# Transposing attention probabilities by halves of the queries, in a kernel that runs a Mamba block beside a local transformer

## The chip, the cores and the metric

The kernel runs on one core of a Trainium2 chip. A core has a matrix engine (TensorE, PE in the profile), a vector engine (VectorE, DVE), an activation engine (ScalarE, ACT), a general engine (GpSimd, POOL) and a sync engine (SyncE, SP) that here issues nearly all transfers. Each engine works through its own queue in order and they meet through semaphores. PE writes to PSUM, eight banks of 512 fp32 columns on 128 partitions; DVE and ACT read and write it[...]. The metric is the device time of one execution in microseconds.

## The reference: what is computed

The input is 4096 tokens of width 256, in fp32. After a layer norm, two independent branches read the same tokens, and the output is their sum with the input:

```
xn = layernorm(x)
x  = x + mamba(xn) + transformer(xn)
```

The Mamba branch widens to 512 channels, convolves over four tokens, and computes for each channel and each of 16 states a linear recurrence over all tokens:

```
h[t] = exp(dt[t]*A) * h[t-1] + dt[t]*xc[t]*B[t]
y[t] = sum over the 16 states of C[t] * h[t]
```

and then `(y + xc*D) * silu(z) @ out_proj`.

The transformer branch has two layers with eight heads of 64. Queries and keys are normalized and rotated. Each window of 128 queries sees its own 128 keys and the 128 before them, under a mask, with a softmax over the at most 256 keys. `attn @ v` and an output projection are added to the stream; a gated GELU network of hidden width 682 follows.

## The kernel before, in words

Everything is fp32. The tokens are cut in 16 steps of 256 for the transformer (so 32 steps over both layers, two windows of 128 in each) and in 8 blocks of 512 for Mamba (four channel groups of 128 in each). One transformer step is the unit of time of the schedule, and one channel group of Mamba runs beside each step.

**The order.** The program first only records its pieces of work with `add(engine, us, emit, reads, writes, soon=...)`. A piece has a key: the step in which it is wanted, less its `soon` (its lead, in steps). `Plan.order` (line 183) then plays all five engines through with the written durations and, on each engine that falls free, picks the ready piece with the smallest key, among those whose key is no more than `AHEAD` steps beyond the oldest piece that isn't done. A piece has to find its buffers free. On PE the planner charges `SWITCH` (0.1) for going from one shape of the array to another (`part`: whole array, "rows" or "columns"), and prefers a piece of the present shape if its key is within `NEAR`. What comes out is one fixed program order for each engine, and so for each queue, SP's among them. `late` in a transfer is its size in KB.

**Mamba's recurrence** (`recur`, line 775) is called for each block b, channel group c and group g of two states, g from 0 to 7. It loads B and C of the two states, broadcast to all partitions, into two tiles of the six-tile buffer `bc` (SP, two transfers of 512 KB). POOL multiplies dt*xc into B for both states at once (line 793). For each state ACT forms the decay in a PSUM tile `da` (line 802), DVE scans (line 807), ACT keeps the last column (line 813), DVE multiplies by C (line 817). Then the states are summed over. If g is in `PAIRED`, POOL adds the two states of the group (line 825) and PE transposes one tile of 128x512 into the bank `y`, as four accumulating 128x128 transposes against the identity (line 829, `collect`). Otherwise PE does so for both states, in eight. `close` (line 842) takes `y` back after all eight groups.

**Attention** (`attend`, line 996) is called for each window, and `pair(g)` in it for each four heads, g being 0 or 1. `score` (line 1017) multiplies queries and keys with the contraction over 64, so heads j = 0 and 1 lie in the upper and the lower half of the array's rows and write to two banks. DVE adds the mask and takes the maximum (line 1032), ACT forms the exponentials and their sums (line 1042). That leaves P with queries on the partitions, in tiles `prs[j]` of 128 queries by two heads (i) by 256 keys. To multiply by V it is needed with the keys on the partitions. So for each i PE transposes four 128x128 pieces into one bank (line 1055), ACT copies the bank to a tile `prT` (line 1059), and after both i `mix` (line 1071) multiplies, with the two heads j in halves of the array's columns. An fp32 product is two matmul instructions on PE; a transpose is one.

PSUM's banks are shared: five for all matmul outputs (`banks`, "mm"), two for the decays, one for `y`.

The rest that the text names: projections L918 and L635, their rotation L945 to L985, the network's matmuls L1176, L1239 and L1258, Mamba's step sizes L734 and output projection L879.

Of the kernel before, what the change touches and what calls it, by code (L numbers as in the profile page):

```python
# [22 lines left out]
ALU = mybir.AluOpType  # L23
# [19 lines left out]
AHEAD = 2.190000  # L43
# [5 lines left out]
PAIRED = (1, 3, 5, 7)  # L49
# [269 lines left out]
def mamba_and_local_transformer(  # L319
# [45 lines left out]
    probs_T = buffer("prT", 4, [P, 2, 2, P])  # L365
# [89 lines left out]
    def load_small():  # L455
        dma(96, lambda: xpw.ap, lambda: xp_wT.rearrange("(c p) n -> p c n", p=P), writes=[xpw], soon=-0.27)
        for at_row in (0, DH):
            dma(32, lambda at_row=at_row: dtw.ap[at_row : at_row + DTR], lambda: dt_wT, writes=[(dtw, at_row)], soon=-1.3)
        dma(128, lambda: b2row.ap, lambda: b2_d[DEPTH - 1 : DEPTH, :].partition_broadcast(P), writes=[b2row], soon=-0.91)

    def load_qkv(l):
        for s in range(3):
            cut = slice(s * INNER, (s + 1) * INNER)
            dma(
                512, lambda cut=cut: wqkv.ap[:, :, cut],
                lambda cut=cut: wqkv_d[l][:, cut].rearrange("(k p) n -> p k n", p=P), writes=[(wqkv, s)], soon=-0.18,
            )

    def load_rest(l):
        dma(512, lambda: wo.ap, lambda: wo_d[l].rearrange("(h p) n -> p h n", p=P), writes=[wo], soon=-0.99)  # L470
        for half in range(2):
            for m, n in ((0, WHOLE), (NM - 1, LAST)):
# [4 lines left out]
                    writes=[(w1, (half, m))], soon=0.35,  # L477
# [4 lines left out]
            lambda: w2_d[l][0:whole, :].rearrange("(m p) n -> p m n", p=MC), writes=[(w2, 0)], soon=-0.25,  # L482
        )
        dma(42, lambda: w2.ap[0 : HID - whole, NM - 1, :], lambda: w2_d[l][whole:HID, :], writes=[(w2, 1)], soon=0.66)
# [28 lines left out]
        add("PE", 8.3, shift, [w1], [pb], soon=-0.7)  # L513
        add("DVE", 0.4, bias, [pb], [b1, b1x], soon=0.6)
        add("DVE", 4.6, scale, [], [w1], port=True, soon=0.34)
# [14 lines left out]
    def base_of(s):  # L530

        base = plan.value(rows_b)
        if s in sums:
            dma(256, lambda: base.ap, lambda: sums[s].ap, [sums[s]], [base], soon=-0.57)
            return base
        dma(256, lambda: base.ap, lambda: rows(x, s), writes=[base], soon=-1.31)
# [3 lines left out]
            ), [b2row], [base], soon=-0.48,  # L540
# [3 lines left out]
    def finish(s, po, base):  # L544

        add("DVE", 0.6, lambda: nc.vector.tensor_tensor(base.ap, halves(po), base.ap, ALU.add), [po], [base], soon=-1.48)  # L546
        if s in sums:
            dma(256, lambda: rows(out, s), lambda: base.ap, [base], soon=-0.51)
            return
        sums[s] = plan.fixed(dram.tile([P, NW, D], F32, tag=f"sum{s}", name=f"sum{s}"))  # L550
        dma(256, lambda: sums[s].ap, lambda: base.ap, [base], [sums[s]], soon=0.0)
# [4 lines left out]
    def shift_column(l, s):  # L556
        now = xts[l, s]
        if s == 0:
            add("POOL", 0.14, lambda: nc.gpsimd.memset(now.ap[:, 1, 0:1], 0.0), [], [(now, 0)], soon=0.0)
        else:  # L560
# [3 lines left out]
                [(old, 1)], [(now, 0)], soon=-0.52,  # L564
            )

    def normalize(s):
# [5 lines left out]
        dma(256, lambda: xb.ap, lambda: rows(x, s), writes=[xb], soon=0.37)  # L573
# [27 lines left out]
        add("DVE", 1.1, stats, [xb], [mv], soon=1.29)  # L601
        add("ACT", 0.5, root, [mv], [rstd], soon=0.53)
        add("DVE", 0.6, centre, [mv, rstd], [xb], port=True, soon=-0.03)
        now = xts[0, s] = plan.value(tokens)
        add("PE", 0.44, turn, [xb], [pt], holds=[now], soon=0.01)
        add("ACT", 0.48, lambda: nc.scalar.copy(now.ap[:, :, 1:], halves(pt)), [pt], [(now, 1)], soon=0.16)
        shift_column(0, s)
        dma(256, lambda: xn_d[s].ap, lambda: now.ap[:, :, 1:], [(now, 1)], [xn_d[s]], soon=-0.93)
# [3 lines left out]
    def reload(s):  # L612
        now = xts[1, s] = plan.value(tokens)
        dma(256, lambda: now.ap[:, :, 1:], lambda: x1_d[s].ap, [x1_d[s]], [(now, 1)], soon=-1.46)
        shift_column(1, s)
# [5 lines left out]
    def in_half(i):  # L621
# [3 lines left out]
            lambda: in_wT[:, i * DI : (i + 1) * DI].rearrange("(k p) n -> p k n", p=P), writes=[w], soon=-1.21,  # L625
# [3 lines left out]
    def in_proj(b, w, c, to):  # L629
# [9 lines left out]
        add("PE", 1.72, emit, [w, xms[b]], [pm], holds=[to], soon=-0.6)  # L639
        return pm  # L640

    def front_load(b):
        xm = xms[b] = plan.value(xms_b)
        for i in range(PB):
            s = b * PB + i
            dma(
                256, lambda i=i: xm.ap[:, :, i * TS : (i + 1) * TS], lambda s=s: xn_d[s].ap, [xn_d[s]], [(xm, i)], soon=0.29
# [5 lines left out]
    def front_conv(b, c, w):  # L653
        xin, xc, tail = plan.value(rows_m), xcs[b], tails[b]
        edge = slice(c * (TAPS - 1), (c + 1) * (TAPS - 1))
        if b == 0:
            add("POOL", 0.14, lambda: nc.gpsimd.memset(xin.ap[:, 0 : TAPS - 1], 0.0), [], [(xin, 0)], soon=0.12)
        else:
# [3 lines left out]
                [(old, c)], [(xin, 0)], soon=0.95,  # L662
            )
        pm = in_proj(b, w, c, xin)
        add("ACT", 0.48, lambda: nc.scalar.copy(xin.ap[:, TAPS - 1 :], pm.ap), [pm], [(xin, 1)], soon=0.73)
        if b < NB - 1:
            add(
                "POOL", 0.14, lambda: nc.gpsimd.tensor_copy(tail.ap[:, edge], xin.ap[:, TB:]), [(xin, 1)], [(tail, c)], soon=0.09
# [5 lines left out]
            ), [], [pm], soon=-0.15,  # L674
# [8 lines left out]
        for j in range(TAPS - 1):  # L683
            add("DVE", 0.7, lambda j=j: tap(j), [xin, pm], [(xc, c) if j == TAPS - 2 else pm], soon=0.78)

    def silu(v):
# [4 lines left out]
        add("ACT", 4.52, emit, [], [v], soon=0.43)  # L691

    def front_dbl(b):
# [3 lines left out]
        def emit():  # L697
# [9 lines left out]
        add("PE", 1.75, emit, [xc, xpw], [px], holds=[xd, part], soon=-0.32, part="columns")  # L707
        add("ACT", 0.48, lambda: nc.scalar.copy(part.ap[0:n, 0:TB], px.ap[DH : DH + n]), [px], [part], alone=[px], soon=0.25)
        add(
            "DVE", 0.6, lambda: nc.vector.tensor_tensor(xd.ap[0:n], px.ap[0:n], part.ap[0:n, 0:TB], ALU.add),  # L710
            [px, part], [(xd, 0)], alone=[px], soon=-1.5,
        )

        add("ACT", 0.48, lambda: nc.scalar.copy(xd.ap[DH : DH + DTR], xd.ap[0:DTR]), [(xd, 0)], [(xd, 1)], soon=-0.07)
        xds[b] = xd
        bc = bcs[b] = plan.fixed(dram.tile([2 * NS, TB], F32, tag=f"bc{b}", name=f"bc{b}"))
        dma(64, lambda: bc.ap, lambda: xd.ap[DTR:n, :], [(xd, 0)], [bc], soon=0.15)

    def gate_conv(b, c, w):
# [4 lines left out]
        add("ACT", 0.48, lambda: nc.scalar.copy(sz.ap[:, c, :], pz.ap), [pz], [(sz, c)], soon=-0.62)  # L724

    def times(b, c):
# [12 lines left out]
        add("PE", 1.15, emit, [xd, dtw], banks2, holds=dts2, soon=0.77, part="rows")  # L739
        for i in range(2):  # L740
# [3 lines left out]
                ), [banks2[i]], [dts2[i]], soon=0.17,  # L744
# [3 lines left out]
    def prepare(b, c):  # L748

        if c % 2 == 0:  # L750
# [7 lines left out]
        add("ACT", 0.6, lambda: nc.scalar.activation(e.ap[:, n], dt.ap, AF.Abs), [dt], [e], soon=-0.79)  # L758
        add("ACT", 0.6, lambda: nc.scalar.activation(dt.ap, dt.ap, AF.Relu), [], [dt], soon=-1.5)
        add("ACT", 0.54, lambda: nc.scalar.activation(e.ap[:, n], e.ap[:, n], AF.Exp, scale=-1.0), [], [e], soon=1.42)  # L760
        add(
            "DVE", 0.36, lambda: nc.vector.tensor_scalar(r.ap[:, n], e.ap[:, n], 1.0, -1.0, ALU.add, ALU.add),
            [e], [r], port=True, soon=0.0,
        )
        add("POOL", 1.22, lambda: nc.gpsimd.tensor_tensor(r.ap[:, n], e.ap[:, n], r.ap[:, n], ALU.subtract), [e], [r], soon=0.43)
        add("ACT", 0.6, lambda: nc.scalar.activation(e.ap[:, n], e.ap[:, n], AF.Ln, bias=one_t), [], [e], soon=0.53)
        add("POOL", 1.22, lambda: nc.gpsimd.tensor_tensor(dt.ap, dt.ap, r.ap[:, n], ALU.add), [r], [dt], soon=-1.5)
        add("POOL", 1.22, lambda: nc.gpsimd.tensor_tensor(dt.ap, dt.ap, e.ap[:, n], ALU.add), [e], [dt], soon=-0.88)
        add(
            "DVE", 0.61, lambda: nc.vector.tensor_tensor(dtx.ap, dt.ap, xc.ap[:, c, :], ALU.mult),  # L770
            [dt, (xc, c)], [dtx], port=True, soon=0.42,
# [3 lines left out]
    def recur(b, c, g):  # L775
# [6 lines left out]
        for s in range(2):  # L782
# [4 lines left out]
                .rearrange("n t -> (n t)").partition_broadcast(P), [bc], [w], soon=-0.78,  # L787
# [7 lines left out]
            ), [dtx], [u], soon=0.16,  # L795
# [618 lines left out]
```

## Time and profile before

| what | value |
|---|---|
| runs | 1903.18 us median of 3 (1902.42 to 1904.25) |
| the profiled execution | 1899.32 us |
| its span, first to last instruction | 1897.5 us |
| granted TensorE clock | 0.993 |
| median matmul record, L829, L1055, L1017 | 273, 273, 272 ns |
| median weight-load record, L829 and L1055 / L1017 | 141 / 188 ns |
| POOL's sum, L825: count, mean | 128, 1287 ns |
| transfer of two states' B or C: size, issue to landing | 512 KB, 4.4 us |

Times come from one profiled execution. A group's row gives the line of the kernel, the engine, the operation, its output and inputs by name, the shape, the count, the time in which at least one of them ran, the mean of one, and the idle time ahead of them on their engine with what ended it. A matmul record lasts from its start to its modelled end; the next one starts before that, so what a matmul costs PE is read from start to start.

### The profile page before, as it was taken

Reading aid. Unit: us, or ns where it says so; the run is one execution under the profiler, and the core shown is the slowest. Engines: PE = TensorE matmul, PEld = TensorE weight load, DVE = VectorE, ACT = ScalarE, POOL = GpSimd, SP = SyncE. Lnnn points to the kernel's source line nnn. Section 1 sums busy time; section 2 is a strip of 40 time slices with the busy share of each in tenths; the row PEclk is TensorE's granted clock in tenths of the full one; section 3 lists DMA queues with packets and bytes.
Section 4 is the critical chain, followed back from the end, with each engine's and each line's share of the span. In section 5 each row is a group of like instructions: output and inputs, shape, how many; then the busy total and the mean of one; then the engine's idle time right before and its main releaser. Section 6 shows DMA issues by size and latency. Waiting matters only on the chain. (4 is left out here: it accounts for less than half of the span.)

```text
span 1897.5 us, 35612 instructions
## 1 busy us (share of the span) xinstructions
PE 1855.4 (98%) x12432; PEld 1423.5 (75%) x12432; DVE 1724.6 (91%) x3190; ACT 1539.9 (81%) x3634; POOL 1410.9 (74%) x1178
## 2 busy tenths in 40 slices
PE   7999999999999999999999999999999999999997
PEld 4777777877777778778778787778777787777786
DVE  6799999999998999989998898998999989998996
ACT  5897988888878788788886888888898878888773
POOL 3676888777877778867787676887768877787874
PEclk9999999999999999999999999999999999999998
DMA  5453655554555455555555644556444564544654
GB/s 188 139 194 114 221 166 180 180 173 166 198 167 182 145 170 194 163 187 185 191 184 191 216 152 162 169 189 222 152 160 163 191 214 159 180 160 155 217 173 144
DMA packets 133956, 334.69 MB, mean 176 GB/s; under 512 B 13468, under 2 KB 57200, under 8 KB 133776
## 3 DMA queue, kind: packets, MB, share of 16 engines
q1 hardware_dynamic: 133488, 332.21, 52.5%
q8 instruction: 98, 1.61, 0.3%
q14 instruction: 82, 0.67, 0.1%
q10 hardware_dynamic: 288, 0.20, 0.0%
HBM read 315.06 MB, written 17.30 MB: 175 GB/s over the span
## 5 line engine op out<-in xcount | busy, mean ns | idle before, releaser
L793 POOL TENSOR_TENSOR bc<-dtx,bc 128x1024 f32<-128x1024 f32 x256 | 606.0, 2369 | 144.1 <-DMA bc<-bc 107.1
L807 DVE TENSOR_TENSOR_SCAN da<-da,state,bc 128x512 f32<-128x512 f32 x448 | 563.5, 1278 | 39.7 <-ACT da L802 21.1
L802 ACT ACTIVATE da<-dt,negA 128x512 f32<-128x512 f32 x512 | 348.3, 693 | 78.4 <-DVE bc L817 74.9
L918 PE MATMUL mm<-wqkv,xt 128*128 128x512 f32 x768 | 355.1, 598 | 1.4 <-DVE top L1032 1.2
L817 DVE TENSOR_TENSOR bc<-da,bc 128x512 f32<-128x512 f32 x512 | 339.0, 678 | 5.7 <-ACT state L813 3.4
L1176 PE MATMUL mm<-hn,w 128*128 128x256 f32 (+1 forms) x1408 | 338.2, 383 | 1.3 <-DVE mlp L1226 0.5
L1176 PEld LDWEIGHTS mm<-hn,w 128*128 128x128 f32 (+1 forms) x1408 | 256.8, 189 | 60.2 <-issue 17.0
L1042 ACT ACTIVATE pr<-pr,top 128x256 f32<-128x256 f32 (+1 forms) x512 | 253.2, 500 | 25.9 <-DVE top L1032 25.6
L918 PEld LDWEIGHTS mm<-wqkv,xt 128*128 128x128 f32 x768 | 139.5, 191 | 133.4 <-issue 120.7
L825 POOL TENSOR_TENSOR bc<-bc 128x512 f32<-128x512 f32 x128 | 164.6, 1287 | 88.0 <-DVE bc L817 86.9
L829 PE MATMUL y<-ident,bc 128*128 128x128 f32 x1536 | 214.9, 277 | 8.8 <-POOL bc L825 8.3
L1032 DVE CUSTOM_DVE_ANT_0 pr<-mm,maskf,nrm 128x256 f32<-128x256 f32 (+1 forms) x512 | 213.1, 474 | 9.5 <-PE mm L1017 9.0
L985 POOL TENSOR_TENSOR turn<-turn,trig 128x512 f32<-128x512 f32 x128 | 162.9, 1293 | 65.7 <-DVE turn L978 57.1
L829 PEld LDWEIGHTS y<-ident,bc 128*128 128x128 f32 x1536 | 175.5, 142 | 46.6 <-issue 20.8
L945 POOL TENSOR_TENSOR turn<-turn,turn 128x512 f32<-128x512 f32 x128 | 164.6, 1286 | 51.3 <-DVE turn L963 50.8
L1017 PEld LDWEIGHTS mm<-kT,qT 64*128 64x128 f32 x2016 | 119.9, 187 | 36.1 <-issue 14.4
L1059 ACT COPY prT<-mm 128x512 f32<-128x512 f32 (+1 forms) x256 | 137.0, 591 | 7.0 <-PE mm L1055 6.3
L1055 PE MATMUL mm<-ident,pr 128*128 128x128 f32 x1008 | 135.7, 278 | 3.8 <-ACT qT L956 1.4
L813 ACT COPY state<-da 128x1 f32<-128x1 f32 x448 | 70.1, 165 | 85.1 <-DVE da L807 70.3
L1017 PE MATMUL mm<-kT,qT 64*128 64x128 f32 x2016 | 136.7, 281 | 0.0
L1071 PE MATMUL mm<-prT,v 128*64 128x128 f32 x2016 | 132.2, 278 | 0.7 <-ACT prT L1059 0.2
L1055 PEld LDWEIGHTS mm<-ident,pr 128*128 128x128 f32 x1008 | 117.6, 144 | 18.9 <-issue 4.9
(132 smaller groups left out, 3444.9 us busy)
## 6 DMA issues: line engine op xcount, KB each, us to landing
bc<-bc SPq DMA_DIRECT2D x512, 512.0 KB, 4.4
io<-in_x SPq DMA_DIRECT2D x32, 256.0 KB, 5.0
mw<-in_in_wT SPq DMA_DIRECT2D x16, 512.0 KB, 5.1
rot<-in_rot SPq DMA_DIRECT2D x32, 128.0 KB, 4.2
xn<-xt SPq DMA_DIRECT2D x16, 256.0 KB, 4.0
xm<-xn SPq DMA_DIRECT2D x16, 256.0 KB, 4.2
x<-mid SPq DMA_DIRECT2D x16, 256.0 KB, 3.0
mw<-in_out_wT SPq DMA_DIRECT2D x8, 512.0 KB, 3.7
```

Of the source, the lines that this page charges most:

```text
L793: "POOL", 2.35, lambda: nc.gpsimd.tensor_tensor(u.ap, dtx.ap.unsqueeze(1).to_broadcast([P, NG, TB]), u.ap, ALU.mult), [dtx], [u], soon=0.16,
L802: "ACT", 0.63, lambda h=h, n=n: nc.scalar.activation(h.ap, dt.ap, AF.Exp, scale=negA[:, c * NS + n : c * NS + n + 1]), [dt], [h], soon=0.96,
L807: "DVE", 1.18, lambda h=h, n=n, i=i: nc.vector.tensor_tensor_scan(h.ap, h.ap, u.ap[:, i, :], state.ap[:, c, n : n + 1] if b else 0.0, ALU. ...
L817: "DVE", 0.61, lambda h=h, i=i: nc.vector.tensor_tensor(u.ap[:, i, :], h.ap, spread[1].ap[:, i, :], ALU.mult), [h, spread[1]], [(u, i)], a ...
L825: add("POOL", 1.22, lambda: nc.gpsimd.tensor_tensor(u.ap[:, 0, :], u.ap[:, 0, :], u.ap[:, 1, :], ALU.add), [], [u], soon=-0.37)
L829: nc.tensor.matmul(y.ap[:, t, :], lhsT=u.ap[:, i, t * P : (t + 1) * P], rhs=ident, is_transpose=True, start=g == 0 and i == 0 and t == 0, ...
L918: nc.tensor.matmul(pm.ap, lhsT=hT[k], rhs=wqkv.ap[:, k, q * INNER : (q + 1) * INNER], start=k == 0, stop=k == KC - 1,)
L1017: nc.tensor.matmul(halves(scs[j])[:, i, a * WIN : (a + 1) * WIN], lhsT=qT.ap[half, 2 * g + i, :], rhs=kk.ap[half, 2 * g + i, :], start=n == 0,
L1032: nc.vector.tensor_tensor_reduce(out=prs[j].ap[:, i, keys], in0=halves(scs[j])[:, i, keys], in1=mask[:, keys], scale=nrm.ap[:, h : h + 1], ...
L1042: nc.scalar.activation(prs[j].ap[:, i, keys], prs[j].ap[:, i, keys], AF.Exp, bias=top.ap[:, h : h + 1], scale=-1.0, accum_out=den.ap[:, h ...
L1055: nc.tensor.transpose(ppv()[:, j, a, :], prs[j].ap[:, i, a * WIN : (a + 1) * WIN], ident)
L1176: nc.tensor.matmul(halves(pm)[0:r, i, :], lhsT=w1.ap[:, k, c0 : c0 + r], rhs=hn.ap[:, k, :], start=k == 0, stop=k == KC - 1,)
```

## The change

Three things change together.

1. **P's transposes.** Both i are done in one piece of work. Each 128x128 transpose is split by the queries, which are P's partitions, in two halves r = 0 and 1. A half takes 64 rows of P against a 64x64 part of the identity and gives 128 keys by 64 queries. The halves lie in different row halves of the array and write to two banks, one for each r. So there are sixteen transposes where there were eight, and the piece is of the shape "rows". ACT copies each bank to its half of the queries in one joint tile `prT`, in runs of 64 columns; that buffer is two tiles of twice the size instead of four.
2. **Six groups.** `PAIRED` holds 0, 1, 3, 4, 5 and 7 instead of 1, 3, 5 and 7.
3. **Leads.** `AHEAD` goes from 2.19 to 2.4, and nearly every `soon` has a new value between -1.5 and 1.5. They change no instruction, only the order.

```diff
-AHEAD = 2.190000
+AHEAD = 2.400000
...
-PAIRED = (1, 3, 5, 7)
+PAIRED = (0, 1, 3, 4, 5, 7)
...
-    probs_T = buffer("prT", 4, [P, 2, 2, P])
+    probs_T = buffer("prT", 2, [P, 2, 2, 2, P])
...
-            add("PE", 1.0, score, [qT] + [kk for _, kk, _ in pieces], scs, holds=prs, soon=0.88, part="rows")
+            add("PE", 1.0, score, [qT] + [kk for _, kk, _ in pieces], scs, holds=prs, soon=0.64, part="rows")
...
-            prTs = []
-            for i in range(2):
-                pp, prT = plan.value(banks), plan.value(probs_T)
-                ppv = lambda pp=pp: pp.ap.rearrange("p (j a q) -> p j a q", j=2, a=2)
-
-                def turn(i=i, ppv=ppv):
+
+            pps, prT = [plan.value(banks) for _ in range(2)], plan.value(probs_T)
+            ppv = lambda r: pps[r].ap.rearrange("p (i j a q) -> p i j a q", i=2, j=2, a=2)
+
+            def turn():
+                for i in range(2):
                     for j in range(2):
                         for a, _, _ in pieces:
-                            nc.tensor.transpose(ppv()[:, j, a, :], prs[j].ap[:, i, a * WIN : (a + 1) * WIN], ident)
-
-                add("PE", 0.44, turn, prs, [pp], holds=[prT], soon=0.02)
+                            for r in range(2):
+                                half = slice(r * DH, (r + 1) * DH)
+                                nc.tensor.transpose(
+                                    ppv(r)[:, i, j, a, :], prs[j].ap[half, i, a * WIN : (a + 1) * WIN], ident[half, half]
+                                )
+
+            add("PE", 0.5, turn, prs, pps, holds=[prT], soon=0.81, part="rows")
+            for r in range(2):
                 add(
-                    "ACT", 0.48, lambda ppv=ppv, prT=prT: nc.scalar.copy(prT.ap[:, :, first:], ppv()[:, :, first:]),
-                    [pp], [prT], soon=0.59,
+                    "ACT", 0.48, lambda r=r: nc.scalar.copy(
+                        prT.ap[:, :, :, first:, r * DH : (r + 1) * DH], ppv(r)[:, :, :, first:, :]
+                    ), [pps[r]], [(prT, r)], soon=1.37,
                 )
 
-                prTs.append(prT)
-
             def mix():
-                for i, prT in enumerate(prTs):
+                for i in range(2):
...
-                                rhs=prT.ap[:, j, a, :],
+                                rhs=prT.ap[:, i, j, a, :],
...
-            add("POOL", 1.22, lambda: nc.gpsimd.tensor_tensor(u.ap[:, 0, :], u.ap[:, 0, :], u.ap[:, 1, :], ALU.add), [], [u], soon=-0.37)
+            add("POOL", 1.22, lambda: nc.gpsimd.tensor_tensor(u.ap[:, 0, :], u.ap[:, 0, :], u.ap[:, 1, :], ALU.add), [], [u], soon=-1.5)
```

## The prediction

> **What bounds the kernel now.** I read the busy shares first, then the busy time by stretch, then the costliest groups, then the matrix engine's timeline around one attention pair, then the waits. Busy time and the forty slices:
>
> ```profile
> PE 1855.4 (98%) x12432; PEld 1423.5 (75%) x12432; DVE 1724.6 (91%) x3190; ACT 1539.9 (81%) x3634; POOL 1410.9 (74%) x1178
> ...
> PE   7999999999999999999999999999999999999997
> ...
> DVE  6799999999998999989998898998999989998996
> ```
>
> PE (TensorE) is full from the second slice to the last but one, so there is no stage to single out: PE time saved anywhere in the middle counts. DVE (VectorE) is close behind it. By stretch (columns: length, busy time with instruction count of PE, PEld, DVE, ACT, POOL, then clock, DMA share, GB/s):
>
> ```profile
> 100.00:500.00 400.00, 392.97 (x2698) 300.24 (x2697) 379.25 (x729) 341.13 (x829) 302.78 (x257) 1.00 0.52 172
> ...
> 900.00:1300.00 400.00, 397.28 (x2631) 305.79 (x2630) 361.27 (x662) 330.50 (x788) 304.76 (x247) 0.99 0.55 182
> ```
>
> Of 400 us DVE is busy 379 in the first and 361 in the other: 95% and 90%. That is the ceiling over every PE saving: if DVE could be driven to 98% everywhere, the stretches from 100 to 1700 us (DVE 1489 us in all) would still take 1520 of their 1600, so no more than some 80 us can be had there.
>
> The groups that the change touches (line, engine, operation, count | busy us, mean ns of one | idle before):
>
> ```profile
> L829 PE MATMUL y<-ident,bc 128*128 128x128 f32 x1536 | 214.9, 277 | 8.8 <-POOL bc L825 8.3
> ...
> L1059 ACT COPY prT<-mm 128x512 f32<-128x512 f32 (+1 forms) x256 | 137.0, 591 | 7.0 <-PE mm L1055 6.3
> L1055 PE MATMUL mm<-ident,pr 128*128 128x128 f32 x1008 | 135.7, 278 | 3.8 <-ACT qT L956 1.4
> ```
>
> The 277 ns is latency from issue to end, and successive matmuls overlap. What one costs is the step from its start to the next one's start, which the timeline of PE gives (start us, length us, line):
>
> ```profile
> 952.94 1.04 PE L829 MATMUL y<-ident,bc 128*128 128x128 f32 x8
> 953.91 1.16 PE L1017 MATMUL mm<-kT,qT 64*128 64x128 f32 x16
> 955.00 0.66 PE L1071 MATMUL mm<-prT,v 128*64 128x128 f32 x8
> 955.59 1.53 PE L829 MATMUL y<-ident,bc 128*128 128x128 f32 x12
> 956.95 5.32 PE L918 MATMUL mm<-wqkv,xt 128*128 128x512 f32 x12
> ```
>
> Within a run of records the start-to-start step of a full 128x128 transpose is 109 ns (median over L829, and over L1055). The scores of L1017 use half the array's rows each. They start in twos, 7 ns apart, and the next two start 112 ns after them: 16 in 8 x 0.112 = 0.893 us, where one after another would be 1.8. So two 64-row matmuls do run side by side here, and so do their weight loads.
>
> The timeline shows a second cost. Eight transposes of L829 should take 8 x 0.109 = 0.87 us, but L1017 starts 0.97 later; L1017 then holds PE for 1.09 instead of 0.893, L1071 for 0.59 instead of 4 x 0.109 = 0.436, and the next L829 takes 1.36 instead of 1.31. Going from whole array to half rows to half columns and back thus cost 0.10 + 0.20 + 0.15 + 0.05 = 0.5 us in three **changes of shape**. Over all records in order of start, I count 368 such changes; against nominal steps the median loss is 0.195 us going into rows and 0.230 going back to the whole array. A separate stretch of row-halved work costs about 0.42 us beside its matmuls. The 144 pieces of such work (128 scores, 16 step sizes of L734) now stand in 102 stretches, 1.41 to a stretch.
>
> **The change, part by part.**
>
> *The transposes of P, removed:* 1008 x 0.109 = 109.9 us of PE. *Added:* 2016 transposes of 64 rows by 128 columns, moving 64 identity columns, in 1008 twos. No row shows such a two. Its nearest row is L1017: the same 64x128 weights in twos, with twice the moving columns, 112 ns. If the columns set the step it is half, 56 ns; if the rate of issue or the loads set it (L1017 never issues four instructions, two loads and two matmuls, faster than in 112), it is 112. The transposes' loads are shorter: their load record is 141 ns in L1055 against 188 in L1017[...]. So I take 60 ns, nearer the low end: 1008 x 0.060 = 60.5 us; ends 56.4 and 112.9.
>
> Here the Trainium skill speaks against the change. Its page "TensorE: Matmul & The Clock Gate", section "Back-to-back issue gap", says that a small matmul has a floor: about 25 ns from start to start, but about 62 ns each where the sequencer's hardware decoding is off. By the 62, sixteen transposes would take 0.99 us a pair against eight at 0.109 = 0.87 now, and the part would lose 128 x 0.12 = 15 us instead of saving 49. The trace's row decides: L1017's sixteen average 56 ns, with 7 between the two of a pair, below that floor, so the 62 isn't in force. By the 25, two take 50, just under the 56 of the columns. The same page, section "LDWEIGHTS (loading the stationary operand)", says that a load takes the time of its columns, however few rows it has. The change therefore doubles the load time. One after another, 16 loads at the 0.107 us that its formula gives for 128 columns are 1.7 us a pair, +107 us in all. In L1017 two loads of 128 columns fit into each 112 ns, so I use the row again.
>
> *Changes of shape, added:* a whole-array transpose stood among other whole-array work for nothing; a half-row one needs the array re-shaped unless another row piece stands beside it. Ends: 0 of the 128 pairs (each falls next to a score) and 128 (each alone). At the present 1.41 to a stretch the 128 would make 91. Some will fall beside scores, which they were never free to do. I take 75: 75 x 0.42 = 31.5 us; ends 0 and 53.8.
>
> *The six groups:* groups 0 and 4 join the paired ones, over 8 blocks x 4 channel groups: 64 times one collect of four L829 transposes goes, 64 x 4 x 0.109 = 27.9 us of PE. GpSimd gets 64 more sums. Their row is L825, 1287 ns: 64 x 1.287 = 82.4 us, so POOL goes from 1411 to 1493 us, still below DVE. Who waits for it:
>
> ```profile
> PE y L829 <- POOL bc L825: 8.3, 3, 3.5
> ...
> DVE da L807 <- POOL bc L793: 12.0, 13, 2.6
> ...
> POOL bc L793 <- DMA bc<-bc: 107.1, 74, 4.9
> POOL bc L825 <- DVE bc L817: 86.9, 42, 6.4
> ```
>
> (us in total, times, longest.) The first line, for 128 sums, becomes 192: +4 us. Behind a sum on POOL's queue stands the next group's product (L793), for which the scan (L807) waits; nothing excludes that each sum delays a scan (82 us), and 0 is the other end. Today 128 sums and all else on POOL cost the scan 12 us; half as many sums more: +5. The cover is the stock of three groups' buffers: the chain from a load's issue (4.4 us) over product (2.4), two scans and their products (about 4), sum (1.3) and collect (0.5) is 12.6 us, and a group comes every 1897.5 / 256 = 7.4, so three last 22 us. Without that slack each sum would put its 1.3 us on the scan.
>
> *Eviction:* still two ACT copies of 512 columns a pair, now written in runs of 64: 591 ns each as L1059; on ACT (81%) a tenth more (14 us) would be hidden. Both wait for the one joint transpose of about 0.5 us instead of 0.44 for the first, and it needs two of the five banks at once; behind it on PE's queue everything waits if the order misjudges that. Taken as 0, ends 0 and +10 (128 x 0.08). The four half-size probability buffers become two of twice the size: nothing.
>
> *Leads, and the limit of 2.4 instead of 2.19 steps:* they re-order every queue, SP's loads and POOL's included, and add no instruction. What they could win is PE's idle time, 1897.5 - 1855.4 = 42 us, of which the first 100 us and the last 48 have some 24; what they could lose isn't bounded by any row. Taken as 0, ends -15 and +20.
>
> **Sum:** -109.9 + 60.5 + 31.5 - 27.9 + 4 + 5 = -36.8, so a span of 1860.7. Around the span lie 1.8 us (1899.3 - 1897.5), so 1862.5 for that execution, which was 3.9 us under the median of the runs: **1866 us**. DVE's 1724.6 us are then 93% of the span, and in the stretch from 100 to 500 some 97%, as full as PE is; that is why I credit nothing for leads.
>
> **Rivals.** *The shape changes cluster away.* If the order puts most transposes next to scores (n = 15 stretches) and POOL's delay stays hidden, PE saves 109.9 - 60.5 - 6 + 27.9 = 71 us, and DVE's ceiling of about 80 hardly lets more through: 1832. For it: the stock of row pieces nearly doubles, from 144 to 272, and stretches of two scores exist already (39 of them). Against: a transpose comes due only after its mask and exponentials, when its score is long past.
>
> *DVE takes over.* PE gives up its time, but DVE with waits for ACT, POOL and PE in its queue does not get above 95% in the middle. The 1600 us stretch becomes 1489 / 0.95 = 1568, with the ends as now: -32. If it stays at 94%, -16, or 1887; with every transpose in its own stretch (another 22 us) it is much the same, 1888. For it: DVE's idle time has many small causes (21 us for ACT's decay, 12 for POOL, 12.5 and 11.4 for PE). I put this case at **1888**. Against: a good part of those waits is for PE, and shrinks with it.
>
> *The twos don't run side by side, and it is slower.* If a two costs 109 ns or more, one matmul after another or issue-bound, the transposes save nothing, and their shape changes are a pure loss: +31.5 - 27.9 + 9 = 13 us, **1916**, with every one alone +35. The point from which this decides: the saving is gone when 1008 x (0.109 - step) equals 31.5 + 9 - 27.9 = 12.6, at a step of 97 ns. For it: no record shows four instructions in less than 112 ns, and the skill's floors. Against: the 7 ns between the two of a pair.
>
> **How the numbers follow.** Likeliest case (1866, its own range 1845 to 1882): 0.50. Clustered, 1832: 0.13. DVE or lone stretches, 1888: 0.19. Not side by side, 1916: 0.18. About 0.2% (3.8 us) is what a measurement can tell from no change. The first two lie wholly on the faster side, the third all but 0.02, and of the last 0.05 falls within 0.2%, 0.13 beyond: faster 0.80, same 0.07, slower 0.13. Half of the clustered case lies below 1832 and some 0.12 above 1908, so the range is 1832 to 1908.
>
> **What would show it.** Right: the new transposes' records step by about 60 ns from two to two, with 7 inside; the PE matmul count rises by 1008 - 256 = 752; PE's stretches of row-halved work rise from 102 to about 177; L825's heir has 192 sums of about 1.29 us, and PE waits for it about 12 us; DVE's share reaches 93%. Wrong: a two at 100 ns or more, stretches above 230 or near 110, scan waits on POOL in the tens of us, or PE's busy share falling well below 97% with DVE no fuller, which would say that the order, and not a unit, sets the time.

## The result, and the profile after

The kernel became slower: 1913.95 us (median of 4, 1913.16 to 1916.57) against 1903.51 before, a ratio of 1.0055 with a 95% interval of 1.0043 to 1.0068. The profiled execution's span is 1912.3 us, 14.8 more than before (some 4 us of these are not in the medians: the execution of before that was profiled was one of the faster ones). My 1866 was wrong, and the time lies above the range.

First the busy shares and slices, of the kernel after:

```profile
PE 1830.8 (96%) x13184; PEld 1359.3 (71%) x13184; DVE 1725.4 (90%) x3190; ACT 1543.8 (81%) x3634; POOL 1482.8 (78%) x1242
...
PE   7999999999999999999989999999999999999986
```

The instruction counts are the forecast ones: 752 more matmuls on PE, 64 more sums on POOL. DVE's work is the same, and its share *fell*, from 91 to 90%. PE is less full than before in a longer span. So nothing took over as a full engine. This is one of the signs of being wrong that I had named: PE's share well below 97% with DVE no fuller. By stretch (columns as before):

```profile
100.00:500.00 400.00, 386.62 (x2817) 285.81 (x2816) 371.20 (x695) 330.42 (x792) 311.33 (x263) 0.99 0.51 167
...
900.00:1300.00 400.00, 388.64 (x2792) 289.09 (x2790) 361.80 (x655) 331.63 (x781) 322.91 (x265) 0.99 0.55 185
```

From 100 to 500 us PE lost 6 us of busy time and VectorE 8: VectorE did not move up to the ceiling that I had set for it.

The groups that changed, of the kernel after (line, engine, operation, shapes, count | busy us, mean ns | idle before):

```profile
L829 PE MATMUL y<-ident,bc 128*128 128x128 f32 x1280 | 180.4, 277 | 19.8 <-POOL bc L825 19.6
...
L1057 PE MATMUL mm<-ident,pr 64*128 64x64 f32 x2016 | 90.4, 229 | 3.4 <-DVE turn L978 1.5 <-ACT pr L1042 1.3 <-DVE mlp L1230 0.3
```

and PE's timeline around one joint piece of transposes (start us, length us, line):

```profile
902.36 0.59 PE L1145 MATMUL mm<-sq,mean_w 128*128 128x256 f32 x2
902.89 0.71 PE L1057 MATMUL mm<-ident,pr 64*128 64x64 f32 x16
903.53 1.15 PE L1075 MATMUL mm<-prT,v 128*64 128x128 f32 x16
904.60 1.98 PE L918 MATMUL mm<-wqkv,xt 128*128 128x512 f32 x4
```

Sixteen half-row transposes hold PE for 903.53 - 902.89 = 0.64 us. By their start times, the two of a pair mostly start 3 or 4 ns apart and the next two 63 ns later (112 after the first two of a piece): 8 x 0.063 = 0.504 us, and the rest belongs to a change of shape. They do run side by side, at the step that I took (60).

**A ledger of PE's time.** I gave every matmul record the time up to the next one's start, and set against it the step of its kind in an unbroken run (whole transpose 109 ns, 256 columns 216, 512 columns 429, half-array work half of its like, a half-row transpose 63 / 2). What a step takes beyond that is put down to a change of shape if it is the step over the change or one of the two after it, else to "elsewhere": waits and other gaps. All in us of one profiled execution:

| kernel | streaming | at changes of shape (number) | elsewhere | before the first and from the last matmul on | span |
|---|---|---|---|---|---|
| before | 1756.6 | 84.3 (361) | 44.4 | 12.2 | 1897.5 |
| after | 1682.3 | 142.3 (578) | 76.2 | 11.5 | 1912.3 |
| difference | -74.3 | +58.0 (+217) | +31.8 | -0.7 | +14.8 |

(My count of 368 changes before had seven more, from the 42-column matmuls of L495, which the ledger takes as whole.) Which three steps count as "at" a change is a choice: with the two steps before a change taken in as well, the differences are +65.6 and +24, with one before and one after it +50.5 and +39. The sum stands; its division is good to some 8 us.

The streaming saved is what I forecast: 109.9 - 63.5 + 27.9 = 74.3 (I had 77.3). Two things ate it: 217 more changes of shape, and waits elsewhere. Stretches of row-halved work went from 102 to 208, where I had taken 177, and those of column-halved work from 90 to 116, of which I had not thought.

### The profile page after: what moved, and what is told of

It is laid out like the page before. It is cut to its first block, busy times and chain, and to the rows that moved or that the text cites. A ratio compares the mean times of both kernels' runs of the same rounds, so it can differ in the third digit from the quotient of the medians.

```text
span 1912.3 us, 37355 instructions
## 1 busy us (share of the span) xinstructions
PE 1830.8 (96%) x13184; PEld 1359.3 (71%) x13184; DVE 1725.4 (90%) x3190; ACT 1543.8 (81%) x3634; POOL 1482.8 (78%) x1242
## 5 line engine op out<-in xcount | busy, mean ns | idle before, releaser
L918 PE MATMUL mm<-wqkv,xt 128*128 128x512 f32 x768 | 362.2, 603 | 3.5 <-DVE turn L965 1.4
L1180 PE MATMUL mm<-hn,w 128*128 128x256 f32 (+1 forms) x1408 | 333.9, 384 | 7.7 <-DVE top L1032 4.2
L825 POOL TENSOR_TENSOR bc<-bc 128x512 f32<-128x512 f32 x192 | 244.4, 1277 | 69.9 <-DVE bc L817 65.6
L1042 ACT ACTIVATE pr<-pr,top 128x256 f32<-128x256 f32 (+1 forms) x512 | 253.3, 500 | 18.2 <-DVE top L1032 17.9
L829 PE MATMUL y<-ident,bc 128*128 128x128 f32 x1280 | 180.4, 277 | 19.8 <-POOL bc L825 19.6
L829 PEld LDWEIGHTS y<-ident,bc 128*128 128x128 f32 x1280 | 144.9, 141 | 54.7 <-POOL bc L825 27.6
L1017 PEld LDWEIGHTS mm<-kT,qT 64*128 64x128 f32 x2016 | 125.7, 189 | 36.0 <-issue 12.4
L1017 PE MATMUL mm<-kT,qT 64*128 64x128 f32 x2016 | 145.1, 284 | 5.6 <-ACT kT L956 2.3
L813 ACT COPY state<-da 128x1 f32<-128x1 f32 x448 | 70.9, 165 | 87.4 <-DVE da L807 71.5
L1075 PE MATMUL mm<-prT,v 128*64 128x128 f32 x2016 | 140.2, 281 | 0.5
L1075 PEld LDWEIGHTS mm<-prT,v 128*64 128x64 f32 x2016 | 113.9, 137 | 27.2 <-issue 8.0
L635 PE MATMUL mm<-xm,mw 128*128 128x512 f32 x256 | 123.2, 608 | 2.0 <-DVE xc L678 1.3
## 6 DMA issues: line engine op xcount, KB each, us to landing
rot<-in_rot SPq DMA_DIRECT2D x32, 128.0 KB, 2.2
```

The source lines that it names most:

```text
L825: add("POOL", 1.22, lambda: nc.gpsimd.tensor_tensor(u.ap[:, 0, :], u.ap[:, 0, :], u.ap[:, 1, :], ALU.add), [], [u], soon=-1.5)
L829: nc.tensor.matmul(y.ap[:, t, :], lhsT=u.ap[:, i, t * P : (t + 1) * P], rhs=ident, is_transpose=True, start=g == 0 and i == 0 and t == 0, ...
L918: nc.tensor.matmul(pm.ap, lhsT=hT[k], rhs=wqkv.ap[:, k, q * INNER : (q + 1) * INNER], start=k == 0, stop=k == KC - 1,)
L1017: nc.tensor.matmul(halves(scs[j])[:, i, a * WIN : (a + 1) * WIN], lhsT=qT.ap[half, 2 * g + i, :], rhs=kk.ap[half, 2 * g + i, :], start=n == 0,
L1042: nc.scalar.activation(prs[j].ap[:, i, keys], prs[j].ap[:, i, keys], AF.Exp, bias=top.ap[:, h : h + 1], scale=-1.0, accum_out=den.ap[:, h ...
L1075: nc.tensor.matmul(hpair(po.ap)[j * DH : (j + 1) * DH, hp, :], lhsT=vv.ap[:, h * DH : (h + 1) * DH], rhs=prT.ap[:, i, j, a, :], start=a == ...
```

## The experiments

**Theory A**: each change of shape costs PE about 0.2 us, and the split pays in them for what it streams less. Against it, **B**: changes hide behind waits and the order's waits took the gain; **C**: GpSimd's 64 more sums did, by late products for the scans; **D**: the leads were set badly, the structure itself is a gain. The expectations also speak of **A+**: A, and a set of leads serves one structure only. Later came **E**: VectorE is the real bound; and **F**: PE, VectorE and the dependences hold each other. Times are medians; the kernel before, run beside each set, stood at 1902.2, 1905.8, 1901.7, 1901.5 and 1902.5 us.

### One cost added: extra changes of shape in the order of before

```diff
                 def turn(i=i, ppv=ppv):
+                    if i == 0:
+                        nc.tensor.transpose(ppv()[:, 0, 1, 0:DH], prs[0].ap[0:DH, 0, WIN:], ident[0:DH, 0:DH])
                     for j in range(2):
```

> The kernel before, its order unchanged, with one extra transpose of 64 rows (0.06 us) put ahead of the first four whole-array transposes of P in each of the 128 pairs; what it writes is overwritten. By the order of PE's work, changes of shape rise from 361 to 613. Theory A (each change of shape costs PE some 0.2 us, and that is where the gain went): 252 x 0.2 + 128 x 0.06 = 58 us more, so about 1960; at least 1940 if PE's own slack takes some. Theory B (changes of shape are hidden behind waits, and the order's waits took the gain): 8 us more at most, 1904 to 1912.

1937.6 us, ratio 1.0173 (1.0149 to 1.0196): 28 to 37 us more, for 4 us of streaming. The ledger: streaming 1760.6, at changes 128.0 (613), elsewhere 34.0. So 252 changes took 43.7 us, 0.17 each, and 10 us of it came out of waits. B falls. A's mechanism stands with a smaller price than I gave it: the time stayed below my "at least 1940". The busy row of this run's page:

```profile
PE 1895.4 (98%) x12560; PEld 1436.5 (74%) x12560; DVE 1729.8 (89%) x3190; ACT 1545.4 (80%) x3634; POOL 1410.8 (73%) x1178
```

Note that 98% is the share of before too: a 64-row transpose and its two changes count as "busy" like useful work.

### The split alone undone, in the order of after

```diff
-                            for r in range(2):
-                                half = slice(r * DH, (r + 1) * DH)
-                                nc.tensor.transpose(ppv(r)[:, i, j, a, :], prs[j].ap[half, i, ...], ident[half, half])
+                            nc.tensor.transpose(ppv(i)[:, j, a, :], prs[j].ap[:, i, ...], ident)
```

> The kernel after with its own order, but P is transposed in whole 128x128 pieces, one bank for each i; leads, six groups and the joint piece stay. Changes of shape fall from 578 to 404, the streaming of the transposes grows by 46 us. Theory A: the two nearly cancel, 174 x 0.2 = 35 to 43 us less against 46 more, so 1914 to 1925. Theory B (changes hidden, PE's time counts): 1955 to 1960. If PE is no longer what sets the time, 1914.

1917.9 us (1916.17 to 1919.45), against 1913.95 for the kernel after (up to 1916.57). The ledger: streaming 1728.7 (+46.4 against after), at changes 105.4 (404; -36.9), elsewhere 71.8 (-4.4). B falls again. With everything else held, order included, the split saves 46 us of streaming, pays 37 for 174 changes, and is worth about 4 us, with ranges that just overlap. The time alone, near 1914, would also fit the third case of the expectation, that PE no longer sets the time.

```profile
PE 1845.0 (96%) x12176; PEld 1396.6 (73%) x12176; DVE 1725.8 (90%) x3190; ACT 1544.0 (81%) x3634; POOL 1482.8 (77%) x1242
```

The run also parts the change in two. It has the whole transposes of before, but the six groups, the joint piece and the order of after:

| part | streaming | at changes | elsewhere | span | forecast |
|---|---|---|---|---|---|
| the split: after, less this run | -46.4 | +36.9 | +4.4 | -5.3 | -17.9 |
| six groups, joint piece, leads: this run, less before | -27.9 | +21.1 | +27.4 | +20.1 | -18.9 |

(What is missing to the span lies at its two ends.) So the split itself did not make the kernel slower. The other part did: I had it at -27.9 + 4 + 5 = -18.9, with nothing for the order.

### The six groups: undone, and their sums shortened

In the first, only `PAIRED` goes back to four groups; its order is made anew by that. In the second the order stays:

```diff
+            many = slice(0, 8 if g in (0, 4) else TB)
-            add("POOL", 1.22, lambda: nc.gpsimd.tensor_tensor(u.ap[:, 0, :], u.ap[:, 0, :], u.ap[:, 1, :], ALU.add), ...)
+            add("POOL", 1.22, lambda: nc.gpsimd.tensor_tensor(u.ap[:, 0, many], u.ap[:, 0, many], u.ap[:, 1, many], ALU.add), ...)
```

> The kernel after with PAIRED 1, 3, 5, 7 again; its leads were set with six groups, so the order changes too. If the six groups' saving on PE of 28 us is real: about 1940. If GpSimd's sums cause the waits: 1900 or less. If the leads fit one structure only, the order gets worse on top: 1940 to 1960.

> The kernel after with its own order; GpSimd's sums of the two added groups (0 and 4) take 8 of the 512 columns, so that part of the states' sum is left out, and POOL has 64 x 1.2 = 77 us less to do. Theory A and a fault of the order alike: the wait of PE for the sums (19.6 us) shrinks to some 10, the time falls by 5 to 12 us, to 1902 to 1909. Theory C (GpSimd's queue took the gain, by late products for the scans): 25 us less or more, below 1890.

Four groups: 1946.8 us, 33 more than after; the ledger has streaming +27.9, changes +2.5, elsewhere -1.8. Here the streaming put back came through whole, in an order made anew. Short sums: 1909.8 us, 4 less, with POOL's busy time down from 1483 to 1415. That is just under the 5 to 12 that I expected, and hardly clear of the noise. C falls: GpSimd's added sums cost some 4 us, where my sum had 4 + 5 = 9. From before to after PE's wait for the sums rose by 11 us, where I had 4 (8.3 to 19.6, forecast 12); with the short sums it is 14.1:

```profile
PE y L829 <- POOL bc L825: 19.6, 16, 6.5
PE mm L950 <- POOL turn L945: 9.6, 9, 3.0
...
DVE da L807 <- POOL bc L793: 15.0, 15, 2.5
...
POOL bc L793 <- DMA bc<-bc: 146.0, 84, 7.8
```

(kernel after, waits of PE, DVE and POOL: us in total, times, longest.) The scan's wait for POOL went from 12.0 to 15.0 only, though POOL's for its loads went from 107 to 146.

### Leads and structures exchanged

Three kernels: before with the leads and limit of after; after with those of before; before with six groups and its own leads.

> The kernel before (whole transposes, four groups) with the leads and the limit of 2.4 of the kernel after. Theory A+ (the shapes took the split's saving; the rest went because a set of leads serves one structure, and the new set is no better an order than the old): PE's waits grow, 1925 to 1950. If the new leads are simply a better order: 1895 or less. If leads hardly matter: 1900 to 1910.

> The kernel after (halves, six groups) with the leads and the limit of 2.19 of the kernel before; the two copies get the lead that they had. Theory A+: the old set doesn't fit the new structure, 1950 to 2000, with 618 changes of shape by the order of the work. If the new leads are what made the kernel slower: 1866 to 1900, near what I had forecast.

> The kernel before with PAIRED 0, 1, 3, 4, 5, 7 and nothing else; the order is made anew with the old leads. If the six groups' 28 us on PE carry through: 1875 to 1885. Theory A+: a re-made order with leads that weren't set for it loses more than that, 1925 to 1950, by waits on PE and not by changes of shape (383 against 361).

1957.4, 2025.2 and 1975.6 us. All are far slower than both kernels, and slower than A+ had them. A set of leads that fits one structure loses 50 to 110 us on another, even where, as in the third, the other has 28 us less for PE to stream and adds nothing but 64 sums. The third once more, for where its time goes:

> The same kernel as in the earlier run of the six groups alone (before with PAIRED 0, 1, 3, 4, 5, 7, old leads), for its profile: 1970 to 1980 again; PE's losses at changes of shape stay near the 84 us of before, and the loss is in waits elsewhere, 44 us there, 130 or more here.

1979.4 us (one execution); the ledger: streaming 1728.7, at changes 108.9 (383), elsewhere 127.3 against 44.4 before. The loss is mainly waits, spread over many lines, none of them long. The first of PE and of DVE in this run:

```profile
PE y L829 <- POOL bc L825: 24.4, 17, 4.4
PE mm L950 <- POOL turn L945: 16.1, 12, 3.6
PE y L829 <- DVE bc L817: 13.3, 6, 3.8
...
DVE mlp L1226 <- PE mm L1176: 26.8, 18, 6.4
DVE turn L965 <- PE mm L918: 23.7, 14, 4.9
```

PE waits for POOL and DVE while DVE waits for PE. That is an order out of step, not a full engine: DVE is at 89% there.

Not all of it is waiting. The granted clock is 0.980 here against 0.993 before. In short stretches it is half, and matmuls then take twice their step. One such stretch (columns as before, the clock is the third number from the end):

```profile
1213.00:1220.00 7.00, 6.01 (x20) 4.42 (x22) 0.56 (x2) 6.92 (x24) 5.42 (x4) 0.52 0.32 108
```

By the trace, matmuls that began at half the clock took 37 us beyond their steps, against 13 in the kernel before; in the kernel after it is 13 too, so the clock has no part in the main result.

### The leads set anew for three structures

The planner's price of a change was raised from 0.1 to 0.15 us (the joint transposes' duration to 0.61), and each structure got a new set of leads, chosen by the planned end. `AHEAD` was free too, and `NEAR` in the first and the third; whole transposes with six groups kept their 0.3.

> The structure of before (whole transposes, four groups), with leads set anew while the order's maker charges 0.15 us for a change of shape instead of 0.1; the same effort of setting goes into the next two. 351 changes of shape. Theory A (the split gives back in changes of shape what it saves, and leads serve one structure): within 1% of before, 1895 to 1915, and not slower than the halves below.

> Whole transposes, six groups, leads set anew for this structure at 0.15 us a change; 356 changes of shape. Theory A: some of the six groups' 28 us on PE comes through once the leads fit, 1885 to 1905, the best of the three. Theory C (six groups themselves cost, by GpSimd): 1915 or more.

> The structure of the kernel after (halves, six groups), leads set anew at 0.15 us a change and 0.61 us for the joint transposes; 559 changes of shape, hardly fewer than the 578 it had. Theory A: slower than whole transposes with six groups by 5 to 20 us, 1900 to 1920. Theory D (the leads of the kernel after were only set at too low a price; the split itself is a gain of 40 us): 1880 or less, and the best of the three.

1925.6, 1910.8 and 1950.8 us. Ledgers:

| kernel | streaming | at changes (number) | elsewhere |
|---|---|---|---|
| whole, four groups | 1756.6 | 86.3 (351) | 66.2 |
| whole, six groups | 1728.7 | 90.6 (356) | 78.4 |
| halves, six groups | 1682.3 | 143.0 (559) | 115.9 |

All three are slower than A had them (1915, 1905 and 1920 at most). With a truer price the halves still have 559 changes, 203 more than whole transposes with six groups, and the kernel is 40 us slower than those. So the changes are not an accident of one set of leads, and nothing here speaks for D. But it isn't excluded. On the very structures of before and after these sets are 24 and 37 us slower than the leads that the two kernels have, and what stands elsewhere differs by 50 us between three sets of equal origin. Of the 40 us some 20 go with the clock: 0.981 in the halves, 0.992 in whole transposes with six groups, and matmuls begun at half the clock took 35 and 15 us beyond their steps. One set for each structure isn't enough to rank them. None beats the kernel before.

### Streaming taken away without its price

Here the order of before is kept. In the first, only each window's own 128 keys are transposed, and the product with V takes that part twice; the second leaves out the second collect of groups 0 and 4 with nothing in its place; the third does both. The first and the third, and two later runs that leave out transposes, also clear the five banks at the start (2.65 us of VectorE, ahead of its first statistics, which start at 4.00 us instead of 3.87).

```diff
-                        for a, _, _ in pieces:
+                        for a, _, _ in pieces[-1:]:
                             nc.tensor.transpose(ppv()[:, j, a, :], ...)
...
-                                rhs=prT.ap[:, j, a, :],
+                                rhs=prT.ap[:, j, 1, :],
```
```diff
         def collect(i):
+            if g in (0, 4) and i == 1:
+                return
```

> The kernel before, its order unchanged, with only the transposes of each window's own keys; those of the 128 keys before are left out, and the products with V take the own keys' part twice. 496 whole-array transposes fewer, 496 x 0.109 = 54 us of PE saved with no change of shape added: the saving I forecast for the split, without its price. If PE's time carries through in this order as I assumed: 40 to 54 us less, 1850 to 1865. If it carries as in the run with the extra row pieces (48 us of PE gave 35): about 1865. Theory E (PE is not what bounds once some 15 us are gone; DVE and the waits hold): 1880 or more.

> The kernel before, its order unchanged, without the second collect of groups 0 and 4 and without any sum in its place, so one state of two is left out there: 28 us of PE saved, nothing asked of GpSimd. PE's time carries through: 20 to 28 us less, 1875 to 1883. Theory E: 10 us or less.

> Both of the two reductions together in the order of before: 82 us of PE saved, parts of the computation left out as there. PE's time carries through up to VectorE's ceiling: 1825 to 1845. Theory E: 1870 or more, hardly below the better of the two alone.

| left out | streaming saved | time against before (95% interval) | at changes | elsewhere |
|---|---|---|---|---|
| half of P's transposes | 54.0 | 0.9959 (0.9944 to 0.9973): -8 us | 87.4 | 90.1 |
| collects of two groups | 27.9 | 0.9961 (0.9949 to 0.9974): -7 us | 88.7 | 62.5 |
| both | 82.0 | 0.9927 (0.9911 to 0.9943): -14 us | 91.1 | 105.3 |

This is the finding that I least expected. PE at 98% gives back between a seventh and a quarter of what is taken off it; the rest turns into waiting. Of the 54 us saved in the first, 46 reappear "elsewhere" (90.1 - 44.4). Pages of the first and of the third:

```profile
PE 1824.9 (96%) x11936; PEld 1372.0 (73%) x11936; DVE 1724.9 (91%) x3195; ACT 1538.6 (81%) x3634; POOL 1411.1 (75%) x1178
```
```profile
PE 1800.8 (96%) x11680; PEld 1341.4 (71%) x11680; DVE 1726.5 (92%) x3195; ACT 1538.2 (82%) x3634; POOL 1409.9 (75%) x1178
```

With 82 us of streaming gone, PE's busy time fell by 55 and its share by two points. A transpose's record lasts 273 ns where the next starts after 109, so a gap of some 0.16 us between two still lies under a record and counts as busy. The Trainium skill warns of this in "Perfetto Trace Analysis", section "Identifying the Most-Contended Engine": matmul busy time is no good measure of how close a kernel is to its limit, and the share of the weight loads, beside the rate of arithmetic, is to be used instead. That share was 75% before, against the 98 that I read as full. The streaming column is plainer still: 1756.6 of 1897.5 us, 93%.

The same in the order of after:

> The kernel after, its order unchanged, with only the transposes of each window's own keys, the products with V taking that part twice: 992 half-row transposes fewer, 496 x 0.063 = 31 us of PE saved, the changes of shape as they were. If PE's time carries through in this order: 22 to 31 us less, 1883 to 1892. If the order's waits set the time there: 10 us less or nothing, 1904 to 1914.

1903.1 us, 11 less for 31 us of streaming; at changes 151.8, elsewhere 87.4. A third comes through there, just beyond what I had for the case that the order's waits set the time.

### VectorE's work taken away

```diff
+            many = slice(0, 32 if g % 2 and i == 0 else TB)
             ... nc.vector.tensor_tensor(
-                    u.ap[:, i, :], h.ap, spread[1].ap[:, i, :], ALU.mult
+                    u.ap[:, i, many], h.ap[:, many], spread[1].ap[:, i, many], ALU.mult
```

alone in the order of before, together with both of PE's reductions, and in the order of after.

> The kernel before, its order unchanged; in 128 of the 512 products with C (L817) VectorE multiplies 32 of the 512 columns and leaves the rest out, some 128 x 0.55 = 70 us less of DVE. Theory E (VectorE bounds, PE has room): 45 us less or more, below 1857. Theory F (PE, VectorE and the order's dependences hold each other; none gives much alone): 10 to 25 us less, 1877 to 1892, as PE's 82 us gave 16. PE alone bounds: nothing.

> The shortened products of VectorE together with both reductions of PE's work of the earlier run, in the order of before: 70 us of DVE and 82 us of PE saved. Theory F: together they give clearly more than the sum of each alone, 55 us less or more, below 1847. Theory E: as VectorE's relief alone. If fixed orders and dependences set the time and no engine does: the sum of the two or less, 1865 or more.

> The kernel after, its order unchanged, with the same shortened products of VectorE, 70 us of DVE less. Theory F: 10 to 30 us less, 1884 to 1904. Theory E: 45 us less or more, below 1869. PE alone bounds there: nothing, 1910 to 1914.

1898.4 us (0.9978, 0.9965 to 0.9990), 1875.3 (0.9855, 0.9841 to 0.9870) and 1906.9. The product in the first of them (minimum, median and maximum ns):

```profile
L818 DVE TENSOR_TENSOR bc<-da,bc x512: 139/678/694, 77.5 to 1883.1; 128x512 f32<-128x512 f32 x128, 128x32 f32<-128x32 f32 x43
```

From start to start a short product takes 98 ns where a whole one takes 597, so 128 of them save 64 us, near the 70 that I had worked out. DVE's busy time fell by less, 41 us alone (1724.6 to 1683.2): records overlap, and some other instructions grew longer (those of L972, 349 to 448 ns each). Of the 64 some 4 came through, in the order of after 7. So VectorE isn't the bound either, and E falls. F's 10 to 25 and 10 to 30 us for these two weren't met either. Together, 82 us of streaming and 64 of products gave 27 us, more than the 4 + 14 of each alone, so the engines do hold each other; but F's "55 or more" wasn't met. Of the third possibility that I named, dependences and a fixed order setting the time by themselves, the size (1865 or more) fits, and the excess over the sum speaks for some mutual hold beside it. The waits of VectorE in the run with both, against those of before:

```profile
DVE da L809 <- ACT da L804: 26.5, 33, 7.0
DVE da L809 <- POOL bc L795: 14.3, 17, 2.7
DVE turn L970 <- PE mm L923: 13.2, 7, 4.9
DVE pr L1037 <- PE mm L1022: 10.1, 24, 1.3
```

They are those of the kernel before, a little longer now (the scan's wait for POOL, 12.0 there, is in the prediction):

```profile
DVE da L807 <- ACT da L802: 21.4, 21, 7.0
DVE turn L965 <- PE mm L918: 12.5, 4, 5.1
DVE pr L1032 <- PE mm L1017: 9.0, 20, 1.7
```

The scan waits for its decay and its product, the rotation for its projection. Which loop of dependences or buffers holds the time is not settled. An order made for the lighter work, which would separate the dependences from the fixed order, was not tried.

## Why the prediction was wrong

- **"PE time saved anywhere in the middle counts"** is the step that failed first. It was read from the nines in PE's slices. Taken away without any price, in a fixed order, 54 us gave 8 and 82 us gave 14, where I counted the whole up to VectorE's ceiling. Added, it did count: the 48 us of the first experiment (44 at changes, 4 of streaming) made the kernel some 33 us slower. My reading, which no run tests: a tuned order is bent around the engine that is nearly full; it has little slack to lose and no work waiting to move up.
- **The transposes' step** was right: 63 ns for a two, 60 forecast, 63.5 us in all for 60.5. The 62 ns for each matmul that I quoted from the Trainium skill would have made it 124, and were rightly set aside. Nor did the estimate of 107 us from its formula for loads come: the loads' busy time fell, from 1423.5 to 1359.3 us.
- **The changes of shape** were the right term, mis-sized. I had 31.5 us, 53.8 at most, for 75 more stretches of rows; it was 58.0 us for 106 more of rows and 26 more of columns. Of these 36.9 are the split's own, the rest came with the new order. The price of a row stretch (0.42 us) was near: the 252 changes added in the first experiment say 0.17 each, 0.35 for a stretch of two. The number failed: I let many transposes fall beside scores. Of the 208 stretches of rows, 139 hold one piece of sixteen matmuls and 48 hold two; before, 47 held one and 39 two.
- **The six groups**: 27.9 us of PE as forecast, and for POOL some 4 us by the short sums instead of 9. But those 27.9 us, too, were counted in full; in the order of before they gave 7.
- **Leads taken as nothing, -15 to +20**: this term, with what else came with the new order, turned the sign. With the split undone in its own order, the kernel still spends 27.4 us more elsewhere and 21.1 more at changes than before, and is 20 us longer with 27.9 us less to stream. Four exchanges of one part without leads of its own cost 33 to 111 us, and three fresh settings left 66, 78 and 116 us elsewhere. So this term is as large as any that I worked out. Of the +31.8 elsewhere 4.4 are the split's own. How the other 27.4 divide between the joint piece, which needs two banks at once (I had 0 to 10 us for that), the added sums, streaming saved that turned into waiting, and the luck of the leads, no run says.
- **The rivals.** The slower one came within 2 us (1916), by luck, with the wrong mechanism: it let the twos not run side by side. Clustering didn't happen. "DVE takes over" was wrong in that no engine took over: DVE's share fell.

With the measured terms in my sum, the changes at 58.0 and everything else left, it would have been -10.3 us: still faster. Only the share that carries through, and the waits of a new order, turn the sign.

## What to carry to other kernels

Before counting a saving on a "98% busy" TensorE, sum the start-to-start steps of its matmuls against their unbroken step: what is left over shows how much of "busy" is waiting and re-shaping. For half-array work, count the stretches it adds, at some 0.35 us each here, before the columns it saves. In a kernel whose engines all run fixed orders, test a saving by leaving the work out in the old order: if that gives a fifth, expect no more unless the order gets better. And when a change comes with a new order, run the old form in the new order as well: here that told the two apart.

## What the runs showed of the hardware that I had not expected

- Four instructions of half-row work (two loads of 64x128, two transposes of 64 columns) pass TensorE every 63 ns; the trace of before showed no more than four in 112.
- In an order otherwise kept, a change of the array's shape costs PE 0.17 us (43.7 us for 252 added) to 0.21 (36.9 us for 174 taken out). With 252 more of them PE's busy share stayed at 98%.
- A VectorE product cut from 512 columns to 32 takes 98 ns from start to start instead of 597, but VectorE's busy time fell by 41 us and not by the 64 that 128 of them save.
